# Deformable sampling on one core: the table and the hats stored as they are read, and weights with a tile's 180 outputs side by side

## The chip, the cores and the metric

One core of a Trainium2 chip. In the profiles PE is its matmul engine (TensorE; PEld its weight loads), DVE VectorE, ACT ScalarE, POOL GpSimd and SP the sync engine, whose queue issues most transfers (in the kernel before all but the 64 row loads of the first stage). The metric is the device time of one execution in microseconds (us). Ratios are the mean time of one kernel's fast runs over that of the other's fast runs of the same rounds, so they are not quite the ratio of the medians that stand beside them.

Times of stages, used throughout, are read from the trace: the *first stage* ends with the first matmul of the sampling, the *sampling* with the last one, the *drain* runs to the first matmul of the 3x3 convolution, and the *convolution* to the end. A *unit* is one branch of one pair of output rows: about 400 in a run, three branches by 2 images by about 67 row pairs.

## The reference, cut

```python
def _branch(x, w_off, w_def, lw, lb, pad, dil):          # dil 1, 9, 12
    off = _conv(x, w_off, pad, dil)                      # 18 channels: 9 taps x (dy, dx)
    y = _deform_dw(x, off, w_def, pad, dil)              # bilinear sampling at 9 taps, depthwise
    return gelu(_ln2d(y, lw, lb))
def layer0(x):                                           # x: (2, 256, 128, 128) f32, group-normed
    out = _ln2d(branch1 + branch2 + branch3 + conv1x1(x), n1_w, n1_b)
    return _ln2d(mlp(out) + out, n2_w, n2_b)
# then x + layer0(gn(x)), then x + conv3x3(gn(x), ternary weights) + bias
```

The kernel turns the bilinear sampling into matmuls. For a tile of 2 rows by 10 columns of outputs, the 128 partitions hold the table's 128 positions around it. A *hat* is the bilinear weight in one direction as a function of position; the product of the y hat and the x hat of an output is a column of the weight matrix A. A tile has 2 rows x 9 taps x 10 columns = 180 such columns.

## The kernel before

The first stage, a group of four rows at a time: load, normalise, transpose into the table, products for the offsets; then hats from the offsets, stored to device memory.

```python
def columns(g):
    xt = pool.tile([P, KC, R, W], F32, name="xa", tag="xa", bufs=4)
    nc.scalar.dma_start(xt, ...rows of group g...)             # on the ACT queue
    ...normalise...
    ts = pool.tile([P, R, C], F32, name="ts", tag="ts", bufs=2)
    ...8 transposes of xt to tpa, two copies to ts...
    nc.sync.dma_start(tv[...].rearrange("r w c -> w r c"), ts) # one table store a group
    for r in range(R):
        ...two matmuls pz <- wz, xa, one copy to zr...
# offsets(G): 54 small matmuls po <- zr, shift.  make_hats(g): 8 transposes pp, then 12 times
# (2 matmuls ph, Abs on ACT to hb, clamp on DVE, stores of hb on the sync queue); hb has 8 buffers
```

The sampling, a unit at a time; three hats loads of each kind with three buffers, three builds:

```python
def load_hats(u):
    for ky in taps(u):
        hy = pool.tile([P, 3, HP], F32, name="hy", tag="hy", bufs=3)
        hx = pool.tile([P, 3, HP], F32, name="hx", tag="hx", bufs=3)
        for h, start, dims in ((hy, 0, [[0, TC], [3 * HP, TR]]),
                               (hx, 3 * TR * HP, [[3 * HP, TC], [0, TR]])):   # rows repeat
            nc.sync.dma_start(..., bass.AP(..., base + start, dims + [[1, 3 * HP]]))  # 3072 B
def build(u, ky):                                        # A: [P, 9, RI, WA], columns innermost
    nc.vector.tensor_tensor(dst, hy, hx, ALU.mult)       # 128 x 768
def sample(u, c):
    for T in range(0, NT, 2):                            # 14 tiles of 10 columns
        for j in range(2):
            nc.tensor.matmul(pm[:, j, 0:n], lhsT=xts[b, Rt][T + j][...],
                             rhs=A[:, m0:m1, AO + (T + j) * CI : AO + (T + j + 1) * CI], ...)
        nc.scalar.copy(ev[...], pm[...])                 # evacuation of two tiles
    if c == KC - 1:
        prepare(u + 2)                                   # builds u + 2, then load_hats(u + 3)
    for ky in kys:
        accumulate(u, c, ev, ky)                         # DVE: ring += defw * ev
```

## Time and profile before

| | before |
|---|---|
| time | 8737.77 us median of 3 (8732.13 to 8741.12) |
| first stage, sampling, drain, convolution | 1304, 5760, 167, 1511 us |
| a unit in the steady sampling | 14.9 us |
| build | 947 ns of 768 columns, 1130 times |
| hats packets of 3072 B | 199 ns, 15.4 GB/s an engine |

The prediction below shows the lines that carry this. Busy times by stretch of the kernel before (stretch, length, busy us and instructions of PE, PEld, DVE, ACT, POOL, clock, DMA share, GB/s), and some waits of the same 200 us:

```profile
320.00:520.00 200.00, 193.48 (x925) 122.90 (x924) 80.33 (x178) 63.14 (x118) 0.00 (x0) 1.00 0.50 146
```

```profile
ACT zr L214 <- PE pz L207: 81.1, 27, 4.8
...
DVE xa L154 <- DMA xa<-in_x: 18.3, 8, 5.9
```

PE has 925 matmuls in 200 us and hardly stands; no wait for a row load is longer than 5.9 us.

### The profile page before, as it was taken

Reading aid. Unit: us, or ns where it says so; the run is one execution under the profiler, and the core shown is the slowest. Engines: PE = TensorE matmul, PEld = TensorE weight load, DVE = VectorE, ACT = ScalarE, POOL = GpSimd, SP = SyncE. Lnnn points to the kernel's source line nnn. Section 1 sums busy time; section 2 is a strip of 40 time slices with the busy share of each in tenths; the row PEclk is TensorE's granted clock in tenths of the full one; section 3 lists DMA queues with packets and bytes.
Section 4 is the critical chain, followed back from the end, with each engine's and each line's share of the span. In section 5 each row is a group of like instructions: output and inputs, shape, how many; then the busy total and the mean of one; then the engine's idle time right before and its main releaser. Section 6 shows DMA issues by size and latency. Waiting matters only on the chain. (4 is left out here: it accounts for less than half of the span.)

```text
span 8742.6 us, 125470 instructions
## 1 busy us (share of the span) xinstructions
PE 8006.7 (92%) x41584; PEld 6024.1 (69%) x41584; DVE 5968.9 (68%) x13113; ACT 4523.6 (52%) x9542; POOL 714.5 (8%) x1292
## 2 busy tenths in 40 slices
PE   5977968899999999999989999999999989999999
PEld 3644637788888888887778888888888854444444
DVE  5334436889888898987688988898888844222222
ACT  1332325566666666666656666666666652122121
POOL 0000000011111111111101111111111110000000
PEclk9978968999999999999999999999999989999999
DMA  7445449999999999997798999999999831111111
GB/s 238 138 144 165 140 140 223 240 243 241 241 236 245 241 244 244 244 236 209 194 240 234 242 241 241 241 240 244 234 248 240 229 97 63 56 58 55 56 58 41
DMA packets 994675, 1661.78 MB, mean 190 GB/s; under 512 B 139424, under 2 KB 540112, under 8 KB 989656
## 3 DMA queue, kind: packets, MB, share of 16 engines
q1 hardware_dynamic: 976600, 1620.03, 69.3%
q10 hardware_dynamic: 17408, 33.56, 1.3%
q8 instruction: 333, 5.46, 0.3%
q14 instruction: 334, 2.74, 0.1%
HBM read 1385.08 MB, written 268.09 MB: 189 GB/s over the span
## 5 line engine op out<-in xcount | busy, mean ns | idle before, releaser
L766 PE MATMUL pm<-A,xs 128*128 128x180 f32 (+2 forms) x22288 | 3893.1, 331 | 430.8 <-ACT ev L775 391.8
L766 PEld LDWEIGHTS pm<-A,xs 128*128 128x128 f32 x22288 | 3636.2, 194 | 651.5 <-ACT ev L775 503.6
L775 ACT COPY ev<-pm 128x360 f32<-128x360 f32 (+2 forms) x5572 | 2305.3, 456 | 1572.8 <-PE pm L766 830.9
L740 DVE SCALAR_TENSOR_TENSOR ring<-ev,defw,ring 128x256 f32<-128x256 f32 (+5 forms) x6272 | 2786.8, 463 | 213.6 <-ACT ev L775 44.4
L1078 PE MATMUL pc<-cring,signs 128*128 128x512 bf16 x6912 | 1502.9, 380 | 4.1 <-ACT cring L1059 3.4
L696 DVE TENSOR_TENSOR A<-hy,hx 128x768 f32<-128x768 f32 x1130 | 1020.0, 947 | 372.3 <-DMA hx<-hats 184.0
L1078 PEld LDWEIGHTS <-signs 128*128 128x128 bf16 x6912 | 671.0, 97 | 835.6 <-issue 7.0
L481 ACT ACTIVATE T<-T,rs 128x256 f32<-128x256 f32 x1280 | 663.6, 595 | 3.3 <-POOL rs L477 3.2
L1090 DVE SCALAR_TENSOR_TENSOR o<-pc,wpn,o 128x512 f32<-128x512 f32 x128 | 96.1, 751 | 676.0 <-PE pc L1078 676.0
L474 POOL TENSOR_SCALAR rs<-mv 128x4 f32<-128x4 f32 x320 | 107.4, 336 | 5225.1 <-DVE mv L472 4274.0
L440 PE MATMUL hp<-T,w 128*128 128x512 f32 x1024 | 489.2, 602 | 7.8 <-ACT T L559 7.8
L1086 ACT ACTIVATE o<-xl,l1b 128x512 f32<-128x512 f32 x128 | 92.2, 721 | 739.0 <-DMA out_x<-o 716.2
L207 PE MATMUL pz<-wz,xa 128*128 128x486 f32 x1024 | 465.7, 580 | 6.3 <-DVE zr L214 3.7
L470 DVE BATCH_NORM_STATS2 st<-T 128x6 f32<-128x256 f32 x1280 | 446.9, 412 | 25.3 <-ACT T L462 25.3
L440 PE MATMUL h<-hT,w 128*128 128x512 f32 x1024 | 460.2, 592 | 0.0
L1059 ACT CAST cring<-rest 128x768 bf16<-128x768 f32 (+1 forms) x256 | 211.8, 828 | 461.1 <-PE pc L1078 295.8
L287 ACT ACTIVATE hb<-ph 108x512 f32<-108x512 f32 x384 | 222.4, 598 | 339.0 <-DMA hats<-hb 222.6
L509 ACT ACTIVATE T<-zc,bb,bw 128x512 f32<-128x512 f32 x384 | 278.7, 780 | 229.2 <-PE zc L493 228.5
L493 PEld LDWEIGHTS zc<-ident,T 128*128 128x128 f32 x2560 | 318.0, 148 | 101.1 <-issue 61.8
L493 PE MATMUL zc<-ident,T 128*128 128x128 f32 x2560 | 361.5, 285 | 19.2 <-ACT T L481 13.8
L476 POOL TENSOR_TENSOR rs<-rs,mhalf 128x4 f32<-128x4 f32 x320 | 370.9, 1159 | 0.0
L462 ACT COPY T<-tp 128x512 f32<-128x512 f32 x640 | 346.7, 605 | 30.9 <-PE tp L460 30.3
(107 smaller groups left out, 5388.6 us busy)
## 6 DMA issues: line engine op xcount, KB each, us to landing
hy<-hats SPq DMA_DIRECT2D x1114, 384.0 KB
hx<-hats SPq DMA_DIRECT2D x1114, 384.0 KB
xs<-table SPq DMA_DIRECT2D x1876, 128.0 KB
g12d<-T SPq DMA_DIRECT2D x128, 512.0 KB
other<-g12d SPq DMA_DIRECT2D x128, 512.0 KB
xl<-x1d SPq DMA_DIRECT2D x120, 384.0 KB
hats<-hb SPq DMA_DIRECT2D x256, 144.0 KB
xa<-in_x ACTq DMA_DIRECT2D x64, 512.0 KB
```

Source lines behind the costliest of these rows:

```text
L207: nc.tensor.matmul(pz[:, 0:NZ], lhsT=xt[:, c, r, :], rhs=k["wz"][:, c, :], start=c == 0, stop=c == KC - 1,)
L440: nc.tensor.matmul(out, lhsT=w, rhs=v, start=i == 0, stop=i == n - 1)
L462: nc.scalar.copy(Tv[:, 2 * h : 2 * h + 2, :].rearrange("p j c -> p (j c)"), tp)
L470: pin(nc.vector.bn_stats(st[:, j, :], Tv[:, j, :]))
L476: nc.gpsimd.tensor_tensor(rs[:, 0, :], rs[:, 0, :], mhalf[:, 0:NB4], ALU.pow)
L481: nc.scalar.activation(Tv[:, j, :], Tv[:, j, :], AF.Identity, scale=rs[:, 0, j : j + 1], bias=rs[:, 1, j : j + 1],)
L493: nc.tensor.transpose(zc[:, j * P : (j + 1) * P], Tv[:, j, c * P : (c + 1) * P], ident)
L696: nc.vector.tensor_tensor(dst, hy[:, :, i0 * W : i1 * W].rearrange("p t (i w) -> p t i w", w=W), hx[:, :, i0 * W : i1 * W].rearrange("p t ...
L740: nc.vector.scalar_tensor_tensor(dst, src, w, dst, ALU.mult, ALU.add)
L766: nc.tensor.matmul(pm[:, j, 0:n], lhsT=xts[b, Rt][T + j][:, c * P : (c + 1) * P], rhs=A[:, m0:m1, AO + (T + j) * CI : AO + (T + j + 1) * C ...
L775: nc.scalar.copy(ev[:, m0:m1, T * CI : (T + 2) * CI].rearrange("p m (t j) -> p t m j", j=CI), pm[:, :, 0:n].rearrange("p t (m j) -> p t m ...
L1078: nc.tensor.matmul(pc, lhsT=signs[:, k, ky * 3 + kx, m * P : (m + 1) * P], rhs=xc[:, i, k, ky : ky + R, kx : kx + W], start=j == 0, stop=j ...
```

## The change

The intent: larger transfers in the sampling (9 KB of hats and 7 KB of table a partition in one run), fewer of them, and matmul operands that lie in one piece. The core of the diff, with cuts marked:

```diff
-    table = dram("table", [HT * WT, C])
+    table = dram("table", [HT * RP, C])          # RP = TC * NT: columns 10 apart lie together
-    hats = dram("hats", [NOFF // 6, NPAIR, NH, RI * W])
+    hats = dram("hats", [3, NR, NRC, 9, HP])     # branch, row tile, hat, tap: as a unit reads it
 ...                                              # columns(g): the table store
-            nc.sync.dma_start(tv[...].rearrange("r w c -> w r c"), ts)
+            for r in range(R):
+                nc.sync.dma_start(bass.AP(tt, place(y + r, 1, 0), ...), ts[w0 : w0 + n * CI, r, :])
+            for T, c, p0, p1 in ((0, 2 * REACH, 0, w0), (n + 1, 0, w0 + n * CI, W)):
+                nc.sync.dma_start(bass.AP(tt, place(y, T, c), ...), ts[p0:p1])
+            nc.sync.dma_start(bass.AP(tt, place(y, 0, CI), ...), bass.AP(tt, place(y, 1, 0), ...))
 ...                                              # load_tiles: 14 loads become 2
-                xt = pool.tile([P, C], F32, name="xs", tag="xs", bufs=20)
+                xt = pool.tile([P, XN, C], F32, name="xs", tag="xs", bufs=XBUFS)
 ...                                              # load_hats: 6 loads become 2, one buffer each
-                hy = pool.tile([P, 3, HP], F32, name="hy", tag="hy", bufs=3)
-                hx = pool.tile([P, 3, HP], F32, name="hx", tag="hx", bufs=3)
+                h = pool.tile([P, 9 * HP], F32, name=name, tag=name, bufs=1)
 ...                                              # build: one of 2304, 72 bytes between elements
+                    [list(Af.ap[0]), [MO // 3 + MO * dil, 3], [1, MO // 3], [MO, W]],
 ...                                              # sample
-                            rhs=A[:, m0:m1, AO + (T + j) * CI : AO + (T + j + 1) * CI],
+                            rhs=A[:, AO + (T + j) * CI : AO + (T + j + 1) * CI, :, m0 : m0 + nm],
-                        pm[:, :, 0:n].rearrange("p t (m j) -> p t m j", j=CI),
+                        pm[:, :, 0:n].rearrange("p t (j m) -> p t m j", j=CI),
 ...
-                "A": [pool.tile([P, 9, RI, WA], F32, name=f"A{i}") for i in range(2)],
+                "A": [pool.tile([P, WA, MO], F32, name=f"A{i}") for i in range(2)],
-VBUFS = 9
+VBUFS = 7                                        # buffers of the tail, to make room
```

## The prediction

The times of a stepping build in it (5.87 us; 4.05 in rival A) are my estimates, not shown by any trace when they were made; so are ACT's doubled or tripled cost of a word read alone and rival D's higher rate.

> **What bounds the kernel now.** I read the page's slices first, then the busy times by stretch, then the groups by form and the waits of one steady millisecond, then the waits of the DMA queue, and last the start times of single matmuls and single packets.
>
> ```profile
> span 8742.6 us, 125470 instructions
> PE   5977968899999999999989999999999989999999
> DVE  5334436889888898987688988898888844222222
> DMA  7445449999999999997798999999999831111111
> ```
>
> Three stages: the offsets, hats and table up to about 1304 us; the sampling, whose matmuls (L766) start between 1303.8 and 7063.8 us; the 3x3 convolution after 7235 us, which the change doesn't touch. The busy times by stretch give one row of each (columns: stretch, length, then busy us and instructions of PE, PEld, DVE, ACT, POOL, then clock, DMA share, GB/s):
>
> ```profile
> 850.00:1300.00 450.00, 370.36 (x1709) 232.16 (x1707) 160.90 (x356) 131.03 (x237) 0.65 (x1) 0.87 0.47 138
> 2500.00:3500.00 1000.00, 944.74 (x5119) 816.54 (x5117) 893.24 (x2039) 676.86 (x1459) 127.49 (x224) 1.00 0.94 242
> 7235.00:8740.00 1505.00, 1500.89 (x6908) 670.36 (x6907) 418.45 (x548) 298.81 (x377) 0.00 (x0) 1.00 0.16 54
> ```
>
> In the sampling three things are nearly full at once: PE 94%, DVE 89%, DMA 94%. By form, same millisecond:
>
> ```profile
> L766 PE MATMUL pm<-A,xs 128*128 128x180 f32 x3782 | 678.5, 335 | 55.3 <-ACT ev L775 55.3
> L775 ACT COPY ev<-pm 128x360 f32<-128x360 f32 x945 | 406.6, 474 | 249.6 <-PE pm L766 156.5 <-DVE ring L740 86.0 <-PE zc L493 2.3
> L740 DVE SCALAR_TENSOR_TENSOR ring<-ev,defw,ring 128x256 f32<-128x256 f32 x513 | 247.6, 483 | 12.0
> L696 DVE TENSOR_TENSOR A<-hy,hx 128x768 f32<-128x768 f32 x201 | 181.5, 952 | 42.3 <-PE pm L766 19.8 <-DMA hx<-hats 10.9 <-DMA other<-g12d 5.7
> L553 DVE TENSOR_TENSOR T<-T,other 128x1024 f32<-128x1024 f32 x12 | 14.7, 1225 | 0.4
> L462 ACT COPY T<-tp 128x512 f32<-128x512 f32 x112 | 60.8, 607 | 0.0
> ```
>
> 201 builds of the weights A, three a unit, are 67 units: 1000 / 67 = 14.93 us a unit. Per unit PE has 944.74 / 67 = 14.10 us, DVE 13.33 (builds 181.5 / 67 = 2.71, the rest 10.62), ACT 10.10. PE waits only 55 us, for evacuations that wait for DVE's accumulation: PE is the bound, DVE right behind. The DMA queue's own waits of that millisecond:
>
> ```profile
> SPq L666 <- DVE A L696: 339.3, 82, 10.7
> SPq L638 <- PE pm L766: 160.2, 220, 4.5
> ```
>
> A hats load waits for the build that frees its buffer, a table load for the matmuls that free its tile. A unit's hats are 6 x 384 KB = 2.36 MB. Packet by packet, a hats packet (3072 B) takes 200 ns on average, 15.4 GB/s an engine, and a run of hats loads moves about 250 GB/s; 2048-byte packets of other tensors take 85 to 95 ns, up to 390 GB/s. So hats take 9.4 of the 14.93 us. They aren't slow by size alone: the 3072-byte packets of the convolution's loads have a median of 121 ns. What is special is that 8 or 16 partitions read the same row (zero steps in the load), which the change keeps.
>
> Matmul starts, read one by one: an fp32 matmul is two records, and in a burst of L766 the distances are 155, 152, 182, 187, 154, 152, 182, 187: the even tile is read at 152 ns for 180 columns, the odd at 182. Full-width reads of the same kernel (128 columns 109, 512 columns 429) give[...] for 180 columns 152.5. So the odd tiles lose 30 ns a record[...].[...]
>
> [...] (1225 - 947 ns for 256 more elements is 1.09 ns each, 113 ns fixed); no run yet shows a stepping destination.[...]
>
> **The change part by part.** *PE.* A tile's 180 weights become contiguous, so odd tiles read like even ones. Saved per pair 30 + 32 = 62 ns, 14 pairs a unit: 0.87 us, PE 14.10 to 13.23.
>
> *DVE, the build.* Three multiplications of 768 become one of 2304. Contiguous that would be 2304 x 1.086 + 113 = 2.62 us, 0.1 saved. But the destination now steps 18 words (72 bytes) at every element, because a column's 18 weights lie together.[...] DVE then has 10.62 + 5.87 = 16.49 us a unit, or 14.67: in the first case more than the whole unit takes today. The build sits in DVE's order between the accumulations, so nothing hides it.
>
> *ACT.* The evacuation now reads PSUM with a step of 18 words. A contiguous element costs (607 - 474) / 152 = 0.9 ns. If a lone word costs double, 360 x 0.9 = 0.32 us more each, 14 a unit, 4.5 us: ACT 14.6, still under DVE's 16.5.
>
> *Hats loads.* Two loads of 1.18 MB with one buffer each, in place of six with three each. Now the first tap reloads while the others are built; after it, no load starts before the whole build is over. The chain is build, then issue and first packet (about 2.2 us: 0.6 to issue, 1.7 to the first packet in the trace), then the load: 5.87 + 2.2 + 9.4 = 17.5 us at today's rate[...]. Table and tail transfers can fill the gap.
>
> *Table loads.* Two of 7 tiles in place of 14 a row pair, all double-buffered: the 160 us of queue waits mostly go, 7 us of issue a row pair too. They weren't on PE's path.
>
> *First stage.* The queue has about 59 transfers a pair of row groups of 34 us, at 0.41 us: 24 us. It gets per group 4 more hats stores (144 KB ones are cut in two), 6 more for the table (4 rows, 2 edges, and a copy in device memory which waits for them): 20 x 0.41 = 8.2 us more a pair, 32.5 of 34, plus that wait; and 46 zero stores an image, 40 us. The hats buffers already wait for stores (ACT hb for DMA, 191 us between 400 and 1300). I take +120 us, of 0 to 300.
>
> *Seven tail buffers for nine.* Counting the tail's steps by its own rule, they never block a ring in either, and the drain needs 88 steps for 70: +20 us.
>
> Sum: a unit goes from 14.93 to about 17.2 us (DVE 16.49 at 96% busy; the hats chain says the same). About 400 units x 2.27 = +900; with 120 and 20, 8738 + 1040 = 9780 us.
>
> **The rivals.** *A: [...]* Build 4.05; unit = 4.05 + the longer of 10.62 and 2.2 + 9.4 = 15.65: +290, in all 9170.[...] *B: the step costs nothing.* Then PE's 13.23 at 95% gives 13.9 to 14.2 a unit, -280, in all 8600; longer runs could add to it. For it: the change was meant to gain, and PE is the bound[...]. *C: ACT pays three times*[...]: 10.10 + 9.1 = 19.2 a unit, 10500. *D: the hats rate rises[...]*: with the slow build it hides behind DVE and changes only 0.3 us a unit, since the repeated rows stay.
>
> **Range and chances.** I give the main case with C 0.6, A 0.27, B 0.13. The weighted mean is about 9460 and the middle of the distribution about 9650, which I predict; 8 in 10 lie between 8900 and 10300. Slower by over 2% is all of the main case and most of A: 0.8. B splits between faster (0.12) and same (0.08, with a weak A).
>
> **What would show it.** Right: the build's row reads 2304 elements at about 5.9 us, DVE is above 95% in the sampling and PE near 77%, waiting for ACT's evacuations that wait for DVE; the matmuls' distances are all 152 to 156. The rate of hats packets (9216 B) stays near 16 GB/s an engine. The first stage ends near 1420 us. Wrong: a build under 3 us (B); an evacuation over 1 us (C); DVE waiting mostly for hats loads with a short build, which makes the one buffer the cause; or a first stage that grows by over 300 us, because the copies hold up the queue.

## The result, and the profile after

The changed kernel takes 11205.58 us (median of 4, 11193.11 to 11213.75) against 8739.44 (median of 4): ratio 1.2821, interval 1.2799 to 1.2843. The prediction had 9650 and a range up to 10300: the direction was right, the size was far off.

| us | before | after | difference | predicted difference |
|---|---|---|---|---|
| first stage | 1304 | 1983 | +679 | +120 |
| sampling | 5760 | 7520 | +1760 | +900 |
| drain | 167 | 177 | +10 | +20 |
| convolution | 1511 | 1511 | 0 | 0 |

The page's slices after. PE no longer holds its nines in the sampling, and neither does anything else:

```profile
span 11191.3 us, 119106 instructions
...
PE   6764765467777777777677677777777777799999
...
DVE  3223222467777777787656778787777776422222
...
PEclk9776776678899989898888898889899988899999
DMA  5335333778888888888777788888888877211111
```

Busy times by stretch, a piece of the first stage and a millisecond of the sampling:

```profile
850.00:1300.00 450.00, 269.99 (x982) 153.37 (x983) 139.49 (x275) 72.08 (x129) 0.69 (x1) 0.70 0.44 132
...
3500.00:4500.00 1000.00, 772.60 (x4040) 657.47 (x4040) 795.83 (x1508) 525.81 (x1152) 83.45 (x176) 0.90 0.81 191
```

PE 77%, DVE 80%, DMA 81%: three engines with a fifth of their time free. I read that as a chain that goes from one to the next in turn, and not as one engine that is full. By form, same millisecond:

```profile
L803 PE MATMUL pm<-A,xs 128*128 128x180 f32 x2968 | 547.6, 341 | 221.2 <-ACT ev L812 220.6
...
L812 ACT COPY ev<-pm 128x360 f32<-128x360 f32 x742 | 310.1, 475 | 447.0 <-DVE ring L772 342.9 <-PE pm L803 80.0 <-PE zc L541 5.4
L730 DVE TENSOR_TENSOR A<-hy,hx 128x2304 f32<-128x2304 f32 x54 | 241.5, 4473 | 184.1 <-DMA hx<-hats 137.4 <-PE pm L803 46.7
```

54 builds are 1000 / 54 = 18.5 us a unit. PE waits for evacuations, these for DVE's accumulation, and DVE, in whose order the build stands before the accumulations, waits for the hats: 137.4 / 54 = 2.5 us a unit. The queue of the loads shows the other half of the ring:

```profile
SPq L707 <- DVE ring L768: 493.7, 52, 11.5
SPq L707 <- DMA hy<-hats: 162.6, 26, 10.3
```

Half of the time the queue stands at the hats load, whose only buffer is free when the build has ended. The wait is put down to an accumulation; since the accumulations follow the build on DVE at once, I read it as the end of the build; packet by packet the trace agrees (below, under a_rows). (Hats packets have now 9216 B and take 668 ns each: 13.8 GB/s an engine, less than before.)

Now the first stage. The same 200 us as shown of the kernel before, and its waits:

```profile
320.00:520.00 200.00, 145.79 (x576) 84.17 (x574) 53.60 (x116) 42.97 (x77) 0.00 (x0) 0.76 0.36 102
```

```profile
ACT zr L261 <- PE pz L254: 112.0, 15, 15.0
DVE xa L159 <- DMA xa<-in_x: 54.1, 7, 13.1
```

PE does 576 matmuls where it did 925, and a row load is now waited for up to 13.1 us. The sync queue, one pair of row groups (start, us, what):

```profile
419.76 0.72 SPq L243 DMA_DIRECT2D table<-table  x1
420.55 39.53 SPq L351 DMA_DIRECT2D hats<-hb  x63
460.18 3.24 SPq L231 DMA_DIRECT2D table<-ts  x4
463.46 0.82 SPq L238 DMA_DIRECT2D table<-ts  x2
464.39 3.20 SPq L231 DMA_DIRECT2D table<-ts  x4
467.71 0.70 SPq L243 DMA_DIRECT2D table<-table  x1
468.45 0.80 SPq L238 DMA_DIRECT2D table<-ts  x2
469.29 0.41 SPq L299 DMA_DIRECT2D offd<-offs  x1
469.81 0.77 SPq L351 DMA_DIRECT2D hats<-hb  x1
475.11 0.72 SPq L243 DMA_DIRECT2D table<-table  x1
```

The granted clock is down too, 0.76 for 1.00; what that adds no run separates. From copy to copy 55.35 us a pair (475.11 - 419.76), where the kernel before has 34.3 between its table stores. The 14 table transfers take 9.5 us of the queue's time; they were 2 of 0.5 us. The gap before the last copy, 4.5 us, is the copy waiting for the stores it reads.

### The profile page after: what moved, and what is told of

It reads as the page before. It is cut to its first block, busy times and chain, and to the rows that moved or that the text cites. A ratio compares the mean times of both kernels' runs of the same rounds, so it can differ in the third digit from the quotient of the medians.

```text
span 11191.3 us, 119106 instructions
## 1 busy us (share of the span) xinstructions
PE 8447.5 (75%) x41584; PEld 6233.1 (56%) x41584; DVE 6715.9 (60%) x12381; ACT 4470.9 (40%) x9542; POOL 609.0 (5%) x1292
## 5 line engine op out<-in xcount | busy, mean ns | idle before, releaser
L803 PE MATMUL pm<-A,xs 128*128 128x180 f32 (+2 forms) x22288 | 4008.6, 338 | 1763.4 <-ACT ev L812 1702.0
L803 PEld LDWEIGHTS pm<-A,xs 128*128 128x128 f32 x22288 | 3736.7, 210 | 2039.7 <-ACT ev L812 1876.0
L812 ACT COPY ev<-pm 128x360 f32<-128x360 f32 (+2 forms) x5572 | 2251.0, 458 | 3448.9 <-DVE ring L772 2568.4
L730 DVE TENSOR_TENSOR A<-hy,hx 128x2304 f32<-128x2304 f32 x398 | 1780.1, 4473 | 1567.6 <-DMA hx<-hats 1207.0
L254 PE MATMUL pz<-wz,xa 128*128 128x486 f32 x1024 | 501.6, 648 | 183.7 <-DVE xa L159 183.7
L326 PE MATMUL ph<-planes,hatw 128*108 128x512 bf16 (+1 forms) x768 | 313.9, 542 | 200.7 <-ACT hb L334 200.3
L254 PEld LDWEIGHTS pz<-wz,xa 128*128 128x128 f32 x1024 | 217.2, 218 | 430.1 <-issue 234.8
L488 PE MATMUL pc<-xn,convw 128*128 128x512 f32 x512 | 277.7, 693 | 213.3 <-ACT xn L580 213.2
L261 ACT COPY zr<-pz 128x486 f32<-128x486 f32 x128 | 72.1, 563 | 888.8 <-PE pz L254 885.2
L335 DVE TENSOR_SCALAR hb<-hb 108x512 f32<-108x512 f32 x384 | 160.4, 424 | 429.3 <-ACT hb L334 372.8
```

The lines of the kernel that those rows point to most:

```text
L254: nc.tensor.matmul(pz[:, 0:NZ], lhsT=xt[:, c, r, :], rhs=k["wz"][:, c, :], start=c == 0, stop=c == KC - 1,)
L326: nc.tensor.matmul(ph[0:HCH], lhsT=k["hatw"][0:n, i, h0 : h0 + HCH], rhs=pl[0:n, i, :], start=i == 0, stop=i == 1,)
L488: nc.tensor.matmul(out, lhsT=w, rhs=v, start=i == 0, stop=i == n - 1)
L730: pin(nc.vector.tensor_tensor(dst, hy, hx, ALU.mult))
L803: nc.tensor.matmul(pm[:, j, 0:n], lhsT=xts[b, Rt][T + j][:, c * P : (c + 1) * P], rhs=A[:, AO + (T + j) * CI : AO + (T + j + 1) * CI, :, m ...
L812: nc.scalar.copy(ev[:, 0 : 3 * nm, T * CI : (T + 2) * CI].rearrange("p m (t j) -> p t m j", j=CI), pm[:, :, 0:n].rearrange("p t (j m) -> p ...
```

## The experiments

Stage times of all, in us (measured as above; "pair" is the time of two row groups in the middle of the first stage):

| kernel | first stage | sampling | unit | build, ns | pair | total |
|---|---|---|---|---|---|---|
| before | 1304 | 5760 | 14.9 | 947 | 34 | 8743 |
| changed | 1983 | 7520 | 18.8 | 4473 | 55 | 11191 |
| a_plain | 1981 | 7037 | 17.4 | 2559 | | 10706 |
| a_taps | 1980 | 6151 | 15.8 | 1601 | | 9819 |
| a_rows | 1986 | 6139 | 15.5 | 4465 | | 9813 |
| b_weights | 1304 | 5982 | 15.5 | 1586 | | 8965 |
| b_align | 1301 | 5689 | 14.8 | 947 | | 8671 |
| b_rows | 1314 | 5727 | 14.9 | 947 | | 8722 |
| b_hats | 1414 | 6950 | 17.6 | 2560 | 36 | 10042 |
| b_table | 1835 | 5892 | 15.5 | 948 | 51 | 9415 |
| a_freecopy | 1971 | 7540 | 18.9 | 4473 | 55 | 11200 |
| a_pool | 1724 | 7534 | 18.8 | 4473 | 55 | 10946 |
| a_split | 2137 | 7520 | 18.8 | 4472 | 58 to 66 | 11347 |
| a_splitp | 1644 | 7517 | 18.8 | 4472 | 33 (columns) | 10851 |

Names with a_ start from the changed kernel, those with b_ from the kernel before. In a_splitp the 33 is the pace of the column products alone; its table stores take about 57 (see there).

### The sampling: is it the build, the load, or their order?

The theory: with one buffer, build, issue and load stand in series. The rivals: DVE is the bound through the longer build; the matmul operands' layout costs elsewhere.

**The storage without the weights' layout (a_plain).** Edit:

```diff
-                "A": [pool.tile([P, WA, MO], F32, name=f"A{i}") for i in range(2)],
+                "A": [pool.tile([P, MO, WA], F32, name=f"A{i}") for i in range(2)],
 (and the three places that read or write A and pm)
```

> The changed kernel with the weights laid out as before (output rows outermost, so the build writes contiguous rows), storage and loads as changed. Chain theory: a unit of the sampling is build + issue and first packet (2.2 us) + hats load (10.7 us at the measured 221 GB/s) in series, since each hats tile has one buffer. The build falls from 4.47 to about 2.6 us and the unit from 18.5 to about 16.6: some 10450 us, DVE still waiting for hats loads. Rival, DVE is the bound and the slow build is its cause: DVE has 10.6 + 2.6 = 13.2 us a unit, the unit falls to about 14.5 and the time to about 9600 us.

Measured: correct, 10707.98 us (median of 2), ratio 1.2252. The sampling is 483 us shorter, and still 1277 longer than before. Of the same millisecond:

```profile
3500.00:4500.00 1000.00, 842.00 (x4312) 721.33 (x4313) 745.02 (x1609) 570.94 (x1236) 90.98 (x192) 0.92 0.87 204
```

```profile
L730 DVE TENSOR_TENSOR A<-hy,hx 128x2304 f32<-128x2304 f32 x57 | 145.9, 2559 | 228.6 <-DMA hx<-hats 175.7 <-PE pm L803 45.5 <-PE tp L508 5.4
```

The build is 1.9 us shorter and DVE is down to 75% busy. The unit is only 1.2 to 1.4 us shorter, and the wait for the hats grows from 2.5 to 3.1 us a unit (175.7 / 57). The time is 258 us above the 10450 that I expected from the chain, and 1108 above the rival's 9600. So DVE's work is not the bound of the changed kernel. This is the first blow to my main case, which had DVE at 96%.

**The weights' layout without the storage (b_weights).** Edit:

```diff
-                [list(Af.ap[0]), [RI * WA + dil, 3], [WA, i1 - i0], [1, W]],
+                [list(Af.ap[0]), [MO // 3 + MO * dil, 3], [1, i1 - i0], [MO, W]],
 (A as [P, WA, MO], and the reads of A and pm as in the change)
```

> The kernel before with the new weights layout alone (three builds of 768 elements a unit, each stepping 72 bytes). Each build should take about 1.56 us (768 x 1.89 ns + 113 ns, from the changed kernel's 4473 ns), DVE has 10.6 + 4.7 = 15.3 us a unit, matmul starts are all 152 to 156 ns apart, and the unit goes from 14.9 to about 16: 9150 us. If the weights layout were the main cause of the loss, it would come over 10000 us; if the faster matmuls paid for it, under 8750.

Measured: correct, 8970.74 us (median of 2), ratio 1.0265.

```profile
2500.00:3500.00 1000.00, 886.47 (x4908) 758.91 (x4908) 955.36 (x1936) 643.81 (x1397) 136.66 (x212) 0.95 0.88 232
```

```profile
L697 DVE TENSOR_TENSOR A<-hy,hx 128x768 f32<-128x768 f32 x195 | 289.2, 1597 | 14.5 <-PE pm L774 14.4
```

Here the main case's mechanism does hold: DVE is the bound at 96% busy, PE falls to 89%. The matmul starts lie 152 and 155 ns apart, as predicted, where the odd tiles had 182 and 187. But the build costs 1.93 ns a column ((1597 - 113) / 768, with the line's mean), 4.79 us for the three of a unit and not the 5.87 of my estimate, and the layout alone costs 222 us of sampling, not 900; the time came out 180 us under the 9150 that I expected of this run.

**Three smaller loads with three buffers each (a_taps).** The changed kernel, its hats loaded and built in three parts of 3 KB:

```diff
-                h = pool.tile([P, 9 * HP], F32, name=name, tag=name, bufs=1)
-                nc.sync.dma_start(h, bass.AP(..., base + start, dims + [[1, 9 * HP]]))
+            for kx in range(3):
+                    h = pool.tile([P, 3 * HP], F32, name=name, tag=name, bufs=3)
+                    nc.sync.dma_start(h, bass.AP(..., base + start + kx * 3 * HP, dims + [[1, 3 * HP]]))
 (and three builds, one of each part)
```

> The changed kernel with hats loaded and built in three parts a unit (runs of 3 KB, three buffers each, as before), same stored layout, same stepping build. Chain theory: loads overlap the builds again, the unit becomes DVE's 10.6 + 4.7 = 15.3 us plus a little, 16 to 16.5: about 10300 us. Rival, the stored placement is slow by itself (221 GB/s whatever the runs) and sets the unit: it stays at 17.5 to 18.5 us, over 10800 us.

Measured: correct, 9815.48 us (median of 2), ratio 1.1231: 1369 us of sampling come back, with the same bytes, the same buffer space (three buffers of a third each) and the same total of build time (3 x 1.60 = 4.80 us, a little more).

```profile
3500.00:4500.00 1000.00, 874.94 (x4827) 751.66 (x4826) 941.59 (x1898) 635.44 (x1373) 135.28 (x208) 0.94 0.92 228
```

```profile
L742 DVE TENSOR_TENSOR A<-hy,hx 128x768 f32<-128x768 f32 x190 | 285.3, 1601 | 24.7 <-PE pm L815 14.8 <-DMA hx<-hats 8.1 <-PE tp L508 1.5
```

The wait for hats before a build has all but gone (8.1 us in the millisecond, 137.4 in the changed kernel), and DVE is now the bound, at 94%. It came out 500 us below my expectation, because I thought that more of the chain would stay.

**Distinct rows (a_rows).** The changed kernel reads 128 neighbouring rows of hats instead of 8 or 16 that repeat. The result is wrong; bytes, runs, instructions and buffers are the same. The edit does two things at once: no row is read by two partitions, and a load covers 128 rows of device memory instead of 8 or 16.

```diff
-                    h, bass.AP(hats[b].tensor, base + start, dims + [[1, 9 * HP]])
+                    h, bass.AP(hats[b].tensor, first, [[9 * HP, P], [1, 9 * HP]])
```

> The changed kernel whose hats loads read 128 neighbouring rows of 9 KB, one for each partition, in place of 8 or 16 rows repeated (a wrong result on purpose). If the repeated rows make the packets slow, the 9216-byte packet falls from 668 ns to about 370, the load from 10.7 to 6 us, and the unit from 18.8 to DVE's bound of 15.1 to 15.7 us: about 9950 us. If long runs or the placement make them slow, packet and time stay (11200 us).

Measured: 9815.59 us (median of 2), ratio 1.1211. A 9216-byte packet takes 384 ns instead of 668 (24.0 GB/s an engine for 13.8), and 1381 us of sampling come back.

```profile
3500.00:4500.00 1000.00, 883.35 (x4899) 758.62 (x4897) 954.74 (x1813) 643.55 (x1394) 143.21 (x216) 0.95 0.69 233
```

```profile
L731 DVE TENSOR_TENSOR A<-hy,hx 128x2304 f32<-128x2304 f32 x64 | 285.7, 4465 | 15.1 <-PE pm L804 14.9 <-issue 0.2
```

Two quite different edits, one of the order and one of the load's length, give back the same 1370 to 1380 us and end at the same bound, DVE at 94 to 95%. A chain in series is what both shorten. The trace of the changed kernel shows it directly. Over the 53 whole rounds from build to build in this millisecond, the mean times are: build 4.47 us, 0.03 to the issue of the load, 1.90 to its first packet, 11.41 to the end of its last packet, 0.95 to the next build, 18.76 in all. In a_plain (56 rounds) they are 2.56, 0.03, 2.56, 11.51 and 0.94, 17.60 in all. With a_rows the load ends after 6.95 us and lies there for 2.93 us before the next build: it is off the path.

Working it out: 16 engines x 13.8 GB/s = 221 GB/s, so the unit's 2.36 MB take 10.7 us if they have the engines alone; 4.47 + 2.2 + 10.7 = 17.4 of the measured 18.5 to 18.8 us. Of the rest, the rounds above put 0.7 in the load itself (11.41 for 10.7) and 0.95 between its last packet and the build, and take 0.3 off the 2.2. That the load is longer because the unit's other transfers share the engines (191 GB/s x 18.5 us = 3.5 MB a unit, of which 2.36 are hats) was not tested.

**Distinct rows before (b_rows).** The same edit in the kernel before. Its output is wrong, which doesn't matter for the time.

```diff
-                            bass.AP(hats[b].tensor, base + start, dims + [[1, 3 * HP]]),
+                            bass.AP(hats[b].tensor, base + start + ..., [[3 * HP, P], [1, 3 * HP]]),
```

> The kernel before with hats loads that read 128 neighbouring rows of 3 KB in place of repeated ones (a wrong result on purpose). If the repeated rows make the packets slow, 3072 bytes fall from 199 ns to about 125. Then, if hats loads set the pace of the kernel before (which the aligned weights suggest, as freeing 7% of PE gave only 0.8%), the unit falls under 14.2 us and the time under 8500; if DVE and PE set it together, the time stays within 1% of 8740 although the DMA share falls from 0.93 to about 0.7.

Measured: 8712.65 us (median of 4), ratio 0.9949 (0.9930 to 0.9968).

```profile
2500.00:3500.00 1000.00, 944.59 (x5119) 818.53 (x5118) 890.52 (x2030) 679.24 (x1458) 125.82 (x221) 0.99 0.72 241
```

A 3072-byte packet falls from 199 to 144 ns and the DMA share from 0.94 to 0.72, yet PE and DVE stay where they were: DMA at 94% did not bound the kernel before, and the repeated rows cost it half a per cent. The same slowness costs the changed kernel 1381 us because there it stands in the chain.

**PE's gain alone (b_align).** The kernel before with the columns of A moved by one word, in rows of 156 words for 152. Counted from the start of its row, the run of ten words that a tile reads began at word 9, 29, ... in the even tiles (152 ns a matmul) and at word 19, 39, ... in the odd ones (182 ns); now it begins at word 10, 30, ... and 20, 40, ...:

```diff
-AO = 9
-WA = 2 * 12 + W
+AO = 10
+WA = 2 * 12 + W + 4
```

> The kernel before with the weights shifted by one element (first tile column at word 10 of a 156-word row, in place of 9 of 152)[...]. Nothing else changes.[...] all matmul starts 152 to 156 ns apart, PE 13.2 us a unit in place of 14.1, the unit about 14.3 since DVE has 13.3: 8480 to 8560 us. Rival, odd tiles are slow for another reason: distances stay 152 and 182 and the time 8740.

Measured: correct, 8672.88 us (median of 4), ratio 0.9918 (0.9901 to 0.9934). In a burst all matmul distances are now 152 to 153 ns: the shift takes away the odd tiles' 30 ns. Why they cost it was not shown. (133 of the millisecond's 3607 distances under 400 ns are about 300; 132 of these lie in stretches of 3.4 us in which the trace shows a granted clock of 0.5.)

```profile
2500.00:3500.00 1000.00, 914.69 (x5157) 793.19 (x5157) 899.15 (x2056) 684.95 (x1475) 130.75 (x228) 0.97 0.91 244
```

```profile
L775 ACT COPY ev<-pm 128x360 f32<-128x360 f32 x951 | 405.7, 472 | 238.8 <-DVE ring L740 120.5 <-PE pm L766 69.9 <-PE hp L440 2.5
```

This is the fastest kernel: 0.8% below the kernel before, clear of noise. I had expected 2 to 3%. What PE no longer computes, it waits for: ACT's wait for DVE's accumulation grew from 86.0 (in the prediction's line) to 120.5 us in the millisecond. With DVE at 90% right behind, PE was a bound only as far as DVE let it be.

### The first stage: table or hats, and how?

**The table part alone (b_table).**

```diff
+            for r in range(R):
+                nc.sync.dma_start(bass.AP(tt, place(y + r, 1, 0), ...), ts[w0 : w0 + n * CI, r, :])
 ...                                      (all of the table's storage and loads; hats and A as before)
-VBUFS = 9
+VBUFS = 7
```

> The kernel before with the table part of the change alone: the table laid out and stored as in the changed kernel (five small stores, the copy inside device memory), read in 7 KB runs; hats and weights as before. The first stage took 1304 us before and 1983 us in the changed kernel. Theory: the table part did all of this (the compiled order of the first stage's instructions on the TensorE queue is the same blocks of 8 transposes, 8 column products, 30 offset products and 24 hat products in a row as in the changed kernel, where the kernel before mixes them two by two), so the first stage takes 1900 to 2000 us. Rival: the hats' stores did it, then 1300 to 1400 us. Sampling should stay at 5760 us, within 60, since the table's reads are a small part of the traffic (a transfer of 0.92 MB in a row tile). Total 9350 to 9480 us by the theory, 8740 to 8850 us by the rival.

**The hats part alone (b_hats).**

```diff
-    hats = dram("hats", [NOFF // 6, NPAIR, NH, RI * W])
+    hats = dram("hats", [3, NR, NRC, 9, HP])
 ...                                      (all of the hats' storage and loads; table and A as before)
```

> The kernel before with the hats part of the change alone: hats stored as they are read, loaded in 9 KB runs into one buffer each, one build a unit; the table and the weights' layout as before. Theory: the hats part does nothing to the first stage, whose order of instructions stays mixed: 1300 to 1400 us (rival: it did the 679 us, then 1900 to 2000). Sampling by the chain of build, issue, load in series, as in the run with plain weights: a build of 2.56 us, 2.2 us to the first packet and a load of 10.7 to 12 us give 15.5 to 17.4 us a unit: 6400 to 7040 us, with 7037 the likelier since that run differs only in the table. Total 9850 to 10100 us.

Measured, one look each, both correct: b_table 9416.52 us, b_hats 10043.98 (beside 8755.92 for the kernel before). First stages 1835 and 1414: the table part costs 531 of the 679 us, the hats part 110. Both lie just outside what I expected (65 us below, 14 above), and on the theory's side. In the sampling the hats part alone costs 1190, within what I expected, and the table part 132, where I had expected at most 60: with table loads in two pieces of 0.92 MB the build waits 64.6 us a millisecond for hats, against 10.9 before.

```profile
L726 DVE TENSOR_TENSOR A<-hy,hx 128x768 f32<-128x768 f32 x195 | 178.5, 954 | 90.3 <-DMA hx<-hats 64.6 <-PE pm L796 25.6
```

The parts nearly add up: weights 222, table 531 + 132 + 11, hats 110 + 1190 + 1 make 2197. The storage with the weights of before against all of the change, 483, is 261 more than the layout alone costs: here the slow build hurt more in the chain than beside it. Together 2458, and the change costs 11191 - 8743 = 2448; that the sum fits so well is partly luck, as the parts give 38 us too little for the first stage (531 + 110 of 679) and 45 too much for the sampling.

**What in the table part?** In the changed kernel the copy waits 4.5 us for its stores. *Without that wait (a_freecopy):* the copy reads rows that were written long before, so its result is wrong.

```diff
-                    tt, place(y, 1, 0), [[NT * C, TC - CI], [RP * C, R], [1, (NT - 1) * C]]
+                    tt, place(0, 1, 0), [[NT * C, TC - CI], [RP * C, R], [1, (NT - 1) * C]]
```

> The changed kernel whose copy in device memory reads rows that were zeroed long before (a wrong result on purpose): the same transfers and bytes, but the copy no longer waits for the stores of its own row group. If the wait of the issuing queue for those stores is what lengthens the first stage, about 10 us of the 51 us a pair of row groups go, and the first stage falls from 1983 to about 1650 us (time about 10870). If it is the number of transfers issued and not the wait, it stays above 1900 us (time above 11100).

Measured: 11198.1 us (median of 2), ratio 1.279, first stage 1971. The wait is not the cause: the prediction's own suspicion ("the copies hold up the queue") falls.

*Table stores on another queue (a_pool):*

```diff
-                nc.sync.dma_start(bass.AP(tt, place(y + r, 1, 0), ...
+                nc.gpsimd.dma_start(bass.AP(tt, place(y + r, 1, 0), ...
 (the two edges and the copy too)
```

> The changed kernel with the table's stores and the copy issued from GpSimd's queue, which is idle in the first stage; right result. Both the wait and the issue time leave the queue of the hats stores. If that queue is what sets the first stage, it falls from 1983 to 1350 to 1450 us and the time to about 10650 us; if the stores themselves or the device memory are slow[...], it stays above 1700 us. The sampling should stay at 7520 us.

Measured: correct, 10940.71 us (median of 2), ratio 1.2496. First stage 1724: 259 of 679 back (I expected 530 to 630; over 1700 was the case of slow stores), and the middle still has 55 us a pair. What comes back lies at the images' ends: 99 us (265 in the changed kernel) between the last column product of the first image and the first one of the second, and 119 (239) between the last of the second image and the sampling. In the middle the GpSimd queue mostly stands waiting for transposed rows (294 us of 350), so the stores were not the bound there. So the 9.5 us that the table's transfers take of the sync queue's time are not the whole cause either.

What differs besides is the order in which each engine takes its instructions of the first stage, as the tool chain compiled it; I read it from the traces. The order of PE's matmuls in four kernels (t: table transposes, Z: column products, o: offset products, P: plane transposes, H: hat products):

```
before    H2 Z1 P8 Z1 H2 Z1 o2 H2 o10 H2 o13 H2 o7 t8 o1 Z1 t8 Z4 H2 Z1 H2 Z2 P3 H2 P5 Z2 H2 Z4 ...
changed   H3 P8 H12 P8 H8 t8 Z8 t8 o30 Z8 H4 P8 H12 P8 H8 t8 Z8 t8 o33 Z8 H4 ...
b_table   H4 P8 H12 P8 H8 t8 Z8 t8 o30 Z8 H4 P8 H12 P8 H8 t8 Z8 t8 o33 Z8 H4 ...
b_hats    o11 H2 o2 Z3 H2 Z2 H2 Z1 P8 Z1 H2 Z1 H6 t16 o14 H2 Z3 H2 Z1 P7 H2 P1 Z3 H2 Z1 ...
```

Before, and with the hats part alone, one group's columns are worked in between the other's hats; with the table part all of a kind stand in a row. And with the table part ACT, in whose queue the row loads stand, issues a load (X) only right before copies (Z) of the column products, two between one block of hats and the next: "H12 t2 X1 Z2 t2 X1 Z2 H12". The trace of b_table shows what this does:

```profile
687.12 1.97 PE L204 MATMUL tpa<-ident,xa 128*128 128x128 f32 x8 [3.62 <-ACT ts L209]
689.12 0.37 ACTq L194 DMA_DIRECT2D xa<-in_x  x1
695.79 1.00 DVE L156 TENSOR_SCALAR xa<-xa,gn_mean,gn_rstd 128x512 f32<-128x512 f32 x2 [12.89 <-DMA xa<-in_x]
...
696.39 4.42 PE L237 MATMUL pz<-wz,xa 128*128 128x486 f32 x5 [7.30 <-DVE xa L156]
```

The transposes end, they free a row buffer, its load is issued, and PE stands 7.3 us until it has landed. PE's order, ACT's order and the sync queue are tied to each other here, so two kernels try to take them apart:

*A second row load for the transposes (a_split),* so that the column products' buffers don't wait for the transposes:

```diff
+            xt = pool.tile([P, KC, R, W], F32, name="xb", tag="xb", bufs=2)
+            nc.gpsimd.dma_start(xt, ...the same rows...)       # normalised again, for the transposes
             ...transposes, table stores...
             xt = pool.tile([P, KC, R, W], F32, name="xa", tag="xa", bufs=4)
             nc.scalar.dma_start(xt, ...)                       # for the column products
```

> The changed kernel, but the column products of the first stage read their rows from a second load of their own (two buffers, its own normalisation, through the GpSimd queue for the transposes' rows), so a row load no longer waits until the table transposes of an earlier group have freed its buffer. The results stay right. In the run with the table part alone, a pair of row groups takes 51 us against 33, and in it TensorE stands 7.3 us for one row load that was issued only when eight transposes had ended, and again some 4 us for the other. Theory (ring: stores on the sync queue free the transposes' buffers, these free the row buffers, and the load's latency lies open): these two waits go, 8 to 11 us of 55 a pair over 32 pairs: first stage from 1983 to 1630 to 1730 us. Rival (the sync queue's own issue time is the bound, 34 us of transfers a pair plus waits): 1900 us or more. Sampling unchanged at 7520.

Measured: correct, 11348.59 us, first stage 2137, 154 *longer*. Both my theory (1630 to 1730) and the form in which I put it fall. The order became still more of a block (t16 o30 Z16), the column products now run 13 us in a row and then not at all for some 53, and the waits moved to the hats buffers and the transposes. Hiding this latency in the blocked order moved the wait to the next link.

*The same, and the table stores on the GpSimd queue (a_splitp).* The row load for the transposes is on the ACT queue in this one.

```diff
-                nc.sync.dma_start(bass.AP(tt, place(y + r, 1, 0), ...
+                nc.gpsimd.dma_start(bass.AP(tt, place(y + r, 1, 0), ...
 (the two edges and the copy too; and the second row load)
```

> The same second row load, and besides the table stores and the copy on the GpSimd queue instead of the sync queue. The compiled TensorE order is then mixed two by two as in the kernel before (8 transposes, then column, offset and hat products in turn), with the changed table, hats and weights untouched. Theory (the 679 us come from the table stores in the sync queue, through their issue time and the order and waits that this brings): the first stage comes back to 1330 to 1450 us. Rival (the order of the instructions does not matter, and the new layouts' stores are slow in themselves): 1650 us or more, as in the run that moved the stores alone (1724). Sampling unchanged at 7520.

Measured: correct, 10852.68 us, first stage 1644. The compiled order is mixed again ("Z2 H2 Z3 H2 Z3 H2 Z4 H2"), and the same 200 us have

```profile
320.00:520.00 200.00, 182.79 (x835) 116.91 (x835) 78.34 (x171) 54.71 (x99) 29.10 (x49) 0.97 0.52 148
```

835 matmuls, against 576 in the changed kernel and 925 before. A pair of column products takes 33 us. But the table does not keep up, now that it has a row load of its own:

```profile
POOL table L231 <- ACT ts L226: 190.5, 7, 29.1
```

Seven groups are transposed and stored in these 200 us, 57 us a pair, where the kernel before does twelve; the GpSimd queue waits 190.5 us for their copies. When the last column product of the first image starts, at 562 us, 17 of its 32 groups have been stored (27 in the kernel before); the last is stored at 909. Once the column products are over, two groups were stored 11 us apart (778 and 789 us), so the stores can be fast; but no run had columns and table at the old pace together, and the rival (1650 us or more, 1644 measured) is not refuted. Neither half of the edit frees the columns alone (a_pool 55, a_split 58 to 66), but this run also moves the second row load to another queue, so it is not just the sum of the two. In a_pool and a_freecopy the order is mixed only in part, with eight column products still in a row, and both have 55. Over the kernels read, the mixed order goes with 33 to 36 us a pair (in a_splitp for the columns only) and the blocked one with 51 to 66. That the order is the mechanism, and not a companion of it, is argued from this and from the waits; no run changed the order and nothing else. But the stage is 1644 and not the 1330 to 1450 that I expected. Nearly all of the rest sits at the two ends: between the last column product of the first image and the first one of the second lie 351 us (174 before), and 266 (155 before) between the last of the second image and the sampling: there come the table groups that were left over, 15 of 32 in each image; and the hats that trail behind, then the second image's statistics loads (16, where before 9 of them had been issued earlier) and its zero fills stand one after the other in the sync queue. That is read from the trace and was not tested by a run. In part the column products' wait has only been moved to the end.

## Why the prediction was wrong, point by point

**What failed.**

*"A unit goes from 14.93 to about 17.2 us (DVE 16.49 at 96% busy; the hats chain says the same)."* This is the step. I worked out two bounds for a unit, DVE 16.49 and the chain 17.5, found them alike, and took DVE as the one that sets the time, though the chain was the longer in my own numbers. Both rested on a build of 5.87 us, which was my estimate. The chain did set it: 18.5 to 18.8 us with DVE 80% busy, shown by a_taps and a_rows, which leave DVE's work and give back 1370 to 1380 of the 1760 us. What is left then, about 380, is near the layout and the table part alone (222 + 132). The sum had a second error: 400 units of the steady 14.93 us are 5972 us, and the sampling took 5760, since before units at the images' borders load and build fewer taps (1130 builds, not 3 x 398). The changed kernel loads and builds all nine for each (398 builds of 2304), and 400 x 18.8 is its 7520. So of the 860 us that the +900 lacks, about 210 are the start that was taken too high and 640 the unit (18.8 for 17.2).

*"PE near 77%"* came true by luck: PE took 14.3 us a unit (772.6 / 54), not 13.23, of a longer unit. The 30 ns of the odd tiles did not become time: 298 of the millisecond's 2757 distances under 400 ns are about 300 ns, all at a granted clock of 0.5, and the mean is 172.5 ns where the kernel before has 170.2.

*The terms of the chain.* The build was 4.47 us and not 5.87 (1.89 ns a column), 1.4 less. The load was 10.7 us at its own rate, 11.4 in the trace, and not 9.4, because I kept the hats' rate ("stays near 16 GB/s an engine") and it fell to 13.8. The fitting total of 17.4 to the predicted 17.5 is luck; the further 1.1 to 1.4 us lie in the longer load and in 0.95 us between its end and the build, which my sum did not have. The sentence "Table and tail transfers can fill the gap" is a likely reason, not a tested one: they go through the same queue, whose packets take 81.0% of the 16 engines' time in this millisecond.

*Rival A* was nearer in its build (4.05) and in its form, build and load in series: "4.05 + the longer of 10.62 and 2.2 + 9.4 = 15.65". With the measured 4.47 and 10.7 the same sum gives 17.4. Its terms were too small, and it stood as the mild case.

*"I take +120 us"* for the first stage: +679. The list of transfers was right in kind (8.2 us a pair more; the queue's issue time in the trace goes from about 24 to 34 us a pair), and so was the worry about the copy's wait, which I named as a sign of being wrong; but that wait is no part of it (a_freecopy). What I had not thought of is that more work in one queue goes with another order of all the others. The middle of the stage went from 34 to 55 us a pair with the blocked order, and the column products back to 33 with the mixed one, while the table stores stayed at 57; 339 of the 679 us are shown to come back with the stores off the sync queue and a second row load. So the step that failed is the cost of the first stage as a list of transfers; that the order is what took its place is argued, not shown, and the rest, at the images' ends, stays open.

**What held.** The odd tiles' matmuls: distances of 152 and 155 ns after the change, where they had 182 and 187. The stepping destination slows the build (4473 ns, and 2559 without the step in a_plain), and where the storage is unchanged DVE does become the bound, at 96% (b_weights). Rival C, slow evacuations, is refuted: 475 ns after with the 72-byte step, 474 before. Rival B, a free step, is refuted by the same 4473 ns. Rival D, a higher rate, is refuted: the longer runs were slower (13.8 GB/s an engine, 15.4 before). The drain, +10 for +20. The DMA engines were far from idle in the changed kernel's sampling (DMA share 0.81), and still the same bytes in three parts, with three buffers each, took 1369 us less than in one (a_taps).

## What to carry to other kernels

When a change makes transfers larger at the price of buffers, add up the ring of one buffer (consume, issue, load) as a sum, with the load at the rate of this access pattern, and compare it with the fullest engine's work. Here the ring was 18.76 us and DVE's work 10.62 + 4.47 = 15.1, and the longer of the two set the pace, 18.5 to 18.8 us a unit. The slow hats loads looked harmless in the kernel before, with the DMA engines 94% busy, because they overlap (half a per cent, b_rows); in the ring the same slowness cost 1381 us (a_rows). And where a scheduler orders the instructions, compare the order of the engines' instructions before and after, also in stages that the change seems to touch only with a few more stores.

## Figures measured on the way

- A build whose destination steps 18 words: 2304 columns took 4473 ns (changed kernel) and 768 took 1597 (b_weights), 1.89 to 1.93 ns a column when 113 ns are taken as fixed. With contiguous rows 2304 took 2559 (a_plain) and 768 took 947 (before).
- ACT's evacuation: the copy of 128x360 took 475 ns with a step of 72 bytes in what it reads (changed kernel) and 474 without (before).
- A matmul's moving operand of 18 runs of ten words: 152 ns when the runs begin at word 9, 29, ... of their rows, 182 ns at word 19, 39, ..., 152 to 153 ns at word 10, 30, ... and 20, 40, .... Moving the operand by that one word took 0.8% off the kernel (b_align).
- Longer runs of repeated rows were not faster here. With rows read by 8 or 16 partitions each, 3072 B took 199 ns (15.4 GB/s an engine) and 9216 B 668 ns (13.8). With 128 distinct neighbouring rows, 3072 B took 144 (21.3; b_rows) and 9216 B 384 ns (24.0; a_rows). But distinct rows alone are not enough: the table's rows, each read by one partition, took 503 ns in runs of 7168 B that lie 14 KB or more apart (14.2; 512 ns in a_rows), and 62 ns (16.5) in the 1024 B runs of the kernel before, 16 of which lie side by side. What makes the difference no run here separates.
- More transfers in one queue went with a blocked compiled order of the other engines' work: 33 to 36 us a pair of row groups in the mixed order (in one of the three only for the column products), 51 to 66 in the blocked one.
